# Four graph layers on one core: layer 0's table as two half precision terms, its destination one-hots in bfloat16, slots found for 64 edge tiles at once

## The chip, the cores and the metric

The kernel runs on one core of one Trainium2 chip. The time is that of one launch on the device, in microseconds (us), the median over several executions. The page of the profile is made from one execution that the hardware profiler recorded. The engines are named as the profile names them: PE does the matmuls (PEld its weight loads), DVE is the vector engine, ACT the scalar engine, POOL the general engine, and SP issues most of the transfers.

## The reference

12500 nodes with 96 features, 200000 edges sorted by destination, four layers one after the other, each followed by a residual and a layer norm. The change touches layer 0 alone:

```python
def _L0_gnn_ref(x, src, dst, W_self, W_neigh, b):
    msg = x[src]
    neigh_sum = jax.ops.segment_sum(msg, dst, num_segments=n)
    deg = jax.ops.segment_sum(jnp.ones(src.shape, x.dtype), dst, num_segments=n)
    h_neigh = neigh_sum / jnp.maximum(deg, 1.0)[:, None]
    return x @ W_self + h_neigh @ W_neigh + b
...
x = _layernorm(x + _L0_gnn_ref(x, src, dst, ...), axis=-1)
x = _layernorm(x + _L1_gnn_ref(x, ..., src, dst), axis=-1)              # two rounds of sums over edges
x = _layernorm(x + _L2_gnn_ref(x, edge_index, edge_attr_96, ...), axis=-1)  # attention over edges
x = _layernorm(x + _L3_gnn_ref(x, src, dst, ...), axis=-1)              # softmax over the edges of a node
```

## The kernel before

Nodes are cut into 98 tiles of 128 (NB) and edges, in the order of their destinations, into 1563 tiles of 128 (NT). For layer 0 the kernel multiplies first and sums later: `l0_nodes` computes x @ W_neigh for every node and keeps it on the chip as a table in bfloat16, each row as three terms (high part, rest, rest of the rest) beside one another, 288 columns (W3). The own part goes to DRAM in float32.

The sums over edges are matmuls with one-hot matrices. For the first 72 node tiles (NS) each edge is given a slot: the slots of a node tile are arranged so that 25 groups (SQ) of 128 slots hold its edges, and so that each run of 32 slots (GR) reads from one tile of the source table. `edge_steps` finds the slots of 32 edge tiles at a time: a scan over the edges (L1005), a batch of 16 small steps (L1021 to L1052), then, for 16 tiles each (CH), one-hots `A` (L1063), `oq` and products `R` (L1065 to L1075), and matmuls that put everything into its place (L1084). The result is copied from PSUM by ACT (`placed`, L1091).

`expand` adds the two halves of a node tile's slots (`lo`, L1098) and sends the row of sources to DRAM, from where it comes back spread over all partitions (`bc`). From that `one_hots` builds the source one-hot `ohT` in fp8, on DVE for even tiles (L1137) and on ACT in two passes for odd ones (L1134, L1135). `destinations` builds the destination one-hot `ohd` in fp8 on DVE (L1122). Both are also written to DRAM by SP's queue, since the later layers load them again instead of building them.

`first_sums` uses them: `gather` multiplies the table's rows by `ohT`, four matmuls of 32 columns of weights for each group of slots, cut further where a row of 288 crosses a PSUM bank (L1222), and ACT casts the result to bfloat16 messages (L1225 for two banks, L1226 for the third). `scatter`, one turn later, multiplies by `ohd` and adds up (L1234). After the last group of a node tile 25 matmuls with a column of ones count the degrees (L1240). `done` reduces the three terms (L1394), copies the degree (L1399), and for four tiles together `l0_stage` finishes the layer and makes the next layer's table.

The last 26 node tiles go by edges instead (`by_edges`): POOL fetches each edge's row by an indirect transfer (L1299), DVE builds one-hots (L1280), PE sums (L1285). They are interleaved with the 72.

The loop in `passes` sets the order in which instructions are traced: a block of slots, node batches, then as many steps of `first_sums` and `by_edges` as the slots allow. In this stage the order on each engine is then chosen when the kernel is built, by a scheduler with estimated durations; at run time every engine and every queue goes through its list in order.

Layers 1 and 3 run in `whole_pass` with the stored one-hots (L1351 gather, L1354 cast, L1360 scatter); the attention has lines of its own, among them L1546, a one-hot in fp8 on ACT, and L1576 and L1578, which take the exponential of 32 values and write 32 scaled values into every 13th place of a tile (`m[:, :n, :, HD]`).

At the end a flag is worked out from the number of edges found and from `over`; where it is set, a general version of the whole kernel runs afterwards.

Of the kernel before, what the change touches and what calls it, by code (L numbers as in the profile page):

```python
# [23 lines left out]
P = 128  # L24
# [499 lines left out]
W3 = 3 * D  # L524
# [8 lines left out]
UE = 4  # L533

# [6 lines left out]
def gnn_fast(  # L541
# [21 lines left out]
    ident_b = const.tile([P, P], BF16, name="ident_b")  # L563
    nc.vector.tensor_copy(ident_b, ident)
# [40 lines left out]
    tabs_d = [dram.tile([NB * P, 2 * D if i else W3], F16 if i else BF16, name=f"tab_d{i}") for i in range(3)]  # L605
# [22 lines left out]
    nc.vector.tensor_add(w_l0[:D, :D], w_l0[:D, :D], ident[:D, :D])  # L628
    w_kvq = weights("w_kvq", [(Wk, bk), (Wv, bv), (Wq, bq)])
# [33 lines left out]
    over = const.tile([P, NB + 4], F32, name="over")  # L663
# [62 lines left out]

    spare = {}
# [15 lines left out]

    def split(work, v, n, to, engine):

        nc.scalar.copy(to[:, :, 0, :], v)
        r = work.tile([P, GB, D], F32, name="sq")
        nc.vector.tensor_sub(r[:, :n, :], v, to[:, :, 0, :])
        engine.tensor_copy(to[:, :, 1, :], r[:, :n, :])
        engine.tensor_sub(to[:, :, 2, :], r[:, :n, :], to[:, :, 1, :])  # L750
# [38 lines left out]
    def l0_nodes(work, psum, pieces):  # L789
# [3 lines left out]
        for g, n in node_batches():  # L793
# [8 lines left out]
            to = pieces[g // CT][:, g % CT : g % CT + n].rearrange("p g (t w) -> p g t w", t=3)  # L802
            for k in range(0, n, 2):
                m = min(2, n - k)
                p = psum.tile([P, 2, 2 * D], F32, name="tp")
                for i in range(m):
                    nc.tensor.matmul(p[:, i, :], xT[:, k + i, :], w_l0, start=True, stop=True)
                nc.vector.tensor_copy(own[:, k : k + m, :], p[:, :m, :D])
                split(work, p[:, :m, D:], m, to[:, k : k + m], nc.vector)
# [177 lines left out]
    def edge_steps(c, work, psum, t0):  # L987

        n2 = min(2 * CH, TS - t0)
        c0 = t0 % BL  # L990

        pr = psum.tile([P, 3, 2 * CH], F32, name="pr")
        for i0 in range(0, n2, CH):
# [7 lines left out]
            cnt = work.tile([P, CH * P], BF16, name="cnt", bufs=1)  # L1001
# [14 lines left out]
        def small(name, dtype=F32, bufs=1):  # L1016
            return work.tile([P, 2 * CH], dtype, name=name, bufs=bufs)[:, :n]
# [6 lines left out]
        full = work.tile([P, 2 * CH + 1], F32, name="full")  # L1024
        if t0:
            nc.vector.tensor_copy(full[:, 0:1], c.full[:, 2 * CH :])
# [28 lines left out]
        for i0 in range(0, n2, CH):  # L1055
# [6 lines left out]
            A = work.tile([P, P, CH], BF16, name="A", bufs=1)  # L1062
            nc.vector.tensor_tensor(A[:, :, :n], c.iota_p[:, :, :n], pb[:, 0, None, :n].to_broadcast([P, P, n]), op=ALU.is_equal)  # L1063
            oq = work.tile([P, 2, SQ, CH], BF16, name="oq", bufs=1)
# [4 lines left out]
            R = work.tile([P, 2, 2 * SQ + 1, CH], BF16, name="R", bufs=1)  # L1069
            for k in range(2):  # L1070
                nc.vector.tensor_mul(
                    R[:, :, k * SQ : (k + 1) * SQ, :n], oq[:, :, :, :n],
# [3 lines left out]
                R[:, :, 2 * SQ, :n], oq[:, :, SQ - 1, :n], c.shi[:, None, cs].to_broadcast([P, 2, n])  # L1076
            )
            for i in range(n):
# [9 lines left out]
                if t == last:  # L1088

                    two = work.tile([P, 2, 2 * SQ + 1], F32, name="placed", bufs=4)  # L1090
# [4 lines left out]
    def expand(work, psum, placed, d):  # L1095

        lo = work.tile([P, 2 * SQ + 1], F32, name="lo", bufs=3)
        nc.vector.tensor_add(lo, placed[d][:, 1, :], placed[d + 1][:, 0, :])  # L1098
# [8 lines left out]
            s, lo[:SPARE, 2 * SQ :], float(P), lo[:SPARE, SQ - 1 : SQ], op0=ALU.mult, op1=ALU.add  # L1107
# [4 lines left out]
        return lo  # L1112
# [6 lines left out]
    def destinations(work, d, lo):  # L1119

        ohd = work.tile([P, SQ, P], FP8, name="ohd", bufs=2)
        nc.vector.tensor_tensor(  # L1122
            ohd, iota_b[:, None, :].to_broadcast([P, SQ, P]), lo[:, SQ : 2 * SQ, None].to_broadcast([P, SQ, P]),
            op=ALU.is_equal, saturate=False,
        )
        nc.sync.dma_start(ohd_d[d], ohd.rearrange("p q e -> p (q e)"))
        return ohd

    def one_hots(work, d, bc):

        o = work.tile([P, SD], FP8, name="ohT0", bufs=2)
        if d % 2:

            nc.scalar.activation(bc, bc, AF.Square, bias=less)  # L1134
            nc.scalar.activation(o, bc, AF.Relu, bias=1.0, scale=-1.0, saturate=False)  # L1135
# [37 lines left out]
    def granule(at, ohs, sp, q, j, half=0):  # L1173

        if q == SQ - 1 and j < 2:
            c = half * SPARE + j * GR
            return (ident_b if sp.dtype == BF16 else ident_h)[:, c : c + GR], sp
# [4 lines left out]
    UN = 5  # L1182
    UW = UN * W3
    BANK = UW // 3

    def pieces_of(i):

        c = i * W3
        while c < (i + 1) * W3:
            e = min((i + 1) * W3, (c // BANK + 1) * BANK)  # L1190
            yield c // BANK, c % BANK, c - i * W3, e - i * W3
            c = e

    def first_sums(work, msgp, psum, at, table, placed, done):


        ones = msgp.tile([P, 1], BF16, name="ones", bufs=1)
        nc.vector.memset(ones, 1.0)
# [13 lines left out]
        def gather(d, q0):  # L1212
            ohs, _, sp = got[d]
            m = msgp.tile([P, UW], BF16, name="msg")
            two = psum.tile([P, 2, 512], F32, name="two")
            one = psum.tile([P, 512], F32, name="one")
            banks = [two[:, 0], two[:, 1], one]
            for i in range(UN):
                for k, c, w0, w1 in pieces_of(i):
                    for j in range(NG):  # L1220
                        a, b = granule(at, ohs, sp, q0 + i, j)
                        nc.tensor.matmul(  # L1222
                            banks[k][j * GR : (j + 1) * GR, c : c + w1 - w0], a, b[:, w0:w1], start=True, stop=True
                        )
# [630 lines left out]
```

## Time and profile before

| | |
|---|---|
| median of 17 runs | 8192.24 us (8169.2 to 8227.15) |
| the profiled execution | 8200.78 us, span of its instructions 8199.0 us |
| mean granted PE clock | 0.724 |
| busy over the span | PE 5017.6 us (61%), DVE 4432.3 (54%), POOL 3786.8 (46%), ACT 2838.8 (35%) |
| layer 0's sums | from about 250 us to 2007 us, where L1351 begins |

A line of a group reads: source line, engine, operation, output <- inputs, shapes, count | busy us, mean ns of one | idle us of the engine just before them, and what ended it. Durations of neighbouring instructions on one engine overlap a little. A line of a stretch reads: its bounds, its length, then busy us (and count) of PE, PEld, DVE, ACT and POOL, the granted PE clock, the DMA share and GB/s; asked for one source line, it shows that line alone.

### The profile page before, as it was taken

To read this page: it belongs to the slowest core of one execution; us is meant where nothing else is said; L and a number is where in the kernel's file an instruction comes from. 1 tells how busy PE (TensorE), PEld (TensorE's weight loads), DVE (VectorE), ACT (ScalarE), POOL (GpSimd) and SP (SyncE) were. 2 spreads that over 40 slices of the span, in tenths; PEclk is the share of its full clock that TensorE was granted. 3 is DMA by queue.
4 is the path that set the end of the run, shared out by engine and by line. 5 is a ranking of instruction groups with operands and counts; after the bars stand their busy time and mean duration, and the time that the engine had idled before them with its cause. 6 is when DMAs were issued, how large, how long until landed. Compare 5 with 4: busy or idle time off the path is not lost.

```text
span 8199.0 us, 140834 instructions
## 1 busy us (share of the span) xinstructions
PE 5017.6 (61%) x56203; PEld 3430.8 (42%) x56203; DVE 4432.3 (54%) x9374; ACT 2838.8 (35%) x5232; POOL 3786.8 (46%) x3641
## 2 busy tenths in 40 slices
PE   4477778776466664666735555555555537666666
PEld 2345555544344442444424444444444423222323
DVE  8367777775233342444536666666666644444445
ACT  0244444444122231332323444444444423222223
POOL 0233445443444425444356666666666634443442
PEclk9677777777677776777856666666666658777778
DMA  3444444444333342344444444444444443223222
GB/s 94 123 137 147 148 148 155 149 148 127 79 95 96 96 127 75 109 112 108 118 114 127 133 133 131 131 131 131 131 130 134 133 121 85 83 83 83 83 82 62
DMA packets 697249, 949.10 MB, mean 116 GB/s; under 512 B 399450, under 2 KB 489645, under 8 KB 696581
## 3 DMA queue, kind: packets, MB, share of 16 engines
q1 hardware_dynamic: 515222, 631.37, 25.3%
q0 software_dynamic: 150624, 295.17, 14.6%
q10 hardware_dynamic: 30735, 13.47, 0.7%
q8 instruction: 443, 7.26, 0.4%
q14 instruction: 225, 1.84, 0.1%
HBM read 804.38 MB, written 135.22 MB: 115 GB/s over the span
## 4 chain that ended last, share of the span: by engine, by line
PE 20%; another core or an unknown queue 15%; DVE 13%; issue 9%; POOL 4%; ACT 1%; DMA 1%; DVEq 0%; SPq 0%; ACTq 0%; POOLq 0%
PE rows L1351 7%; PE acc L1360 5%; POOL kv L1518 4%; PE acc L1285 3%; DVE ohe L1595 2%; DVE s L1565 2%; DVE sc L1567 2%; DVE mh L1589 2%; PE acc L1611 2%; PE ep L1556 2%; DVE s L1564 1%; DVE msg L1354 1%; PE tp L1467 1%; DVE m L1579 1%
## 5 line engine op out<-in xcount | busy, mean ns | idle before, releaser
L1518 POOL DMA_INDIRECT kv<-kv_d,cols x1563 | 1570.8, 1005 | 875.4 <-issue 444.8
L1299 POOL DMA_INDIRECT rows_e<-tab_d,cols x1257 | 1390.9, 1107 | 872.3 <-PE acc L1285 514.1
L1351 PE MATMUL rows<-tab,ohT 128*32 128x192 f16 (+1 forms) x19992 | 1029.8, 303 | 1065.8 <-issue 689.8
L1354 ACT CAST msg<-rows 128x768 f16<-128x768 f32 (+1 forms) x1320 | 810.8, 639 | 2261.5 <-remote 1274.6
L1354 DVE CAST msg<-rows 128x768 f16<-128x768 f32 x660 | 630.4, 955 | 1776.3 <-remote 932.8
L1351 PEld LDWEIGHTS <-ohT 128*32 128x32 fp8e4 x19992 | 503.6, 102 | 1532.0 <-issue 1484.7
L1611 PE MATMUL acc<-mh,ohe 128*128 128x208 f16 x3115 | 518.4, 333 | 975.8 <-DVE ohe L1595 799.7
L1360 PE MATMUL acc<-msg,ohd 128*128 128x192 f16 (+1 forms) x5100 | 815.5, 301 | 123.7 <-issue 121.7
L1299 POOL DMA_INDIRECT rows_e<-ex_d,cols x611 | 590.2, 966 | 602.7 <-PE acc L1285 428.9
L1611 PEld LDWEIGHTS <-ohe 128*128 128x128 bf16 x3115 | 360.4, 134 | 1078.7 <-DVE ohe L1595 856.8
L1556 PE MATMUL ep<-w_e,attr 97*128 97x96 f32 x3126 | 625.8, 358 | 52.8 <-issue 42.0
L1360 PEld LDWEIGHTS <-ohd 128*128 128x128 fp8e4 x5100 | 446.4, 106 | 442.9 <-issue 391.0
L1556 PEld LDWEIGHTS ep<-w_e,attr 97*128 97x128 f32 x3126 | 585.3, 274 | 67.6 <-issue 61.0
L1576 ACT ACTIVATE ex<-sc 128x32 f32<-128x32 f32 x391 | 89.6, 229 | 1423.7 <-DVE sc L1568 1197.0
L1285 PE MATMUL acc<-rows_e,ones_e 128*128 128x192 f16 (+2 forms) x3660 | 513.7, 293 | 27.4 <-DVE ones_e L1280 17.8
L1225 ACT CAST msg<-two 128x960 bf16<-128x960 f32 x360 | 344.9, 958 | 460.2 <-PE two L1222 255.1
L1564 DVE TENSOR_TENSOR s<-ep,kv 128x384 f32<-128x384 f32 x391 | 215.7, 552 | 527.1 <-remote 366.4
L1158 POOL DMA_INDIRECT spare<-tab_d,spare_i x72 | 124.4, 1728 | 718.7 <-DMA rowd<-lorow 248.7
L1285 PEld LDWEIGHTS <-ones_e 128*128 128x128 bf16 x3660 | 371.8, 116 | 133.0 <-DVE ones_e L1280 24.7
L1565 DVE TENSOR_TENSOR s<-s,qp 128x384 f32<-128x384 f32 x391 | 216.5, 554 | 385.0 <-remote 287.0
L1560 PE MATMUL qp<-qs,ohq 128*128 128x96 f16 x3126 | 312.2, 244 | 182.4 <-issue 181.3
L1167 POOL DMA_INDIRECT spare<-tab_d,spare x72 | 69.3, 962 | 757.2 <-PE rows L1351 610.6
(922 smaller groups left out, 8651.4 us busy)
## 6 DMA issues: line engine op xcount, KB each, us to landing
ohT<-ohT_d SPq DMA_DIRECT2D x204, 400.0 KB
ohd<-ohd_d SPq DMA_DIRECT2D x204, 400.0 KB
attr<-cols_edge_attr_dram SPq DMA_DIRECT2D x390, 192.0 KB
bc<-rowd SPq DMA_DIRECT2D x72, 800.0 KB
qb<-qrow SPq DMA_DIRECT2D x97, 512.0 KB
sb<-srow SPq DMA_DIRECT2D x72, 512.0 KB
cb<-crow SPq DMA_DIRECT2D x72, 512.0 KB
ohd_d<-ohd SPq DMA_DIRECT2D x72, 400.0 KB
```

The source lines that it names most:

```text
L1225: nc.scalar.copy(m[:, : 2 * BANK].rearrange("p (b w) -> p b w", b=2), two[:, :, :BANK])
L1285: nc.tensor.matmul(acc[:, : W + count], ones[:, :, i], rows_of[u][:, i, : W + count], start=(t + i == first), stop=(t + i == last),)
L1299: nc.gpsimd.indirect_dma_start(out=m[:, i, :W], out_offset=None, in_=table, in_offset=bass.IndirectOffsetOnAxis(ap=rest_src[:, t : t + 1], ...
L1351: nc.tensor.matmul(ps[j * GR : (j + 1) * GR, i // R, i % R * W : (i % R + 1) * W], a, b, start=True, stop=True)
L1354: (nc.scalar.copy if engine else nc.vector.tensor_copy)(m, ps[:, :, : R * W])
L1360: nc.tensor.matmul(acc[d][:, :W], got[d][1][:, q, :], m, start=(q == 0), stop=(q == SQ - 1))
L1518: nc.gpsimd.indirect_dma_start(out=kv[:, i, :], out_offset=None, in_=kv_d, in_offset=bass.IndirectOffsetOnAxis(ap=cols[:, t0 + i : t0 + i ...
L1556: nc.tensor.matmul(ep[:, i, :], a[:, i * P : (i + 1) * P], w_e, start=True, stop=True)
L1560: nc.tensor.matmul(qp[:, i, :], ohq[:, i * P : (i + 1) * P], qs[:, t * D : (t + 1) * D], start=(t == 0), stop=(t == 1))
L1564: nc.vector.tensor_mul(s[:, :n, :], ep[:, :n, :], kv[:, :n, :D])
L1565: nc.vector.tensor_mul(s[:, :n, :], s[:, :n, :], qp[:, :n, :])
L1611: nc.tensor.matmul(acc[d].rearrange("p t w -> p (t w)"), ohe[:, k * P : (k + 1) * P, i], m[:, i].rearrange("p t w -> p (t w)"), start=(t = ...
```

## The change

The table of layer 0 becomes two terms in half precision (192 columns, `halves_of`), after W_neigh is multiplied by 64 (L0); the degree's reciprocal takes the factor out. `split` goes. ACT sums the squares of each row into `l0_ss`, and at the end the flag is also set where such a sum lies below 1 and is not 0, or is 2^30 or more.

`gather` takes four groups of slots at a time, then two, in turn, into PSUM tiles of two banks and of one, with one ACT cast each into message tiles that have a column of ones behind each row; `scatter` then counts the degrees in the same matmul (193 columns). The degree is copied by ACT.

`destinations` compares in bfloat16, five groups of slots (QG) at a time, the group innermost, and the scatter reads its weights from there at steps of five elements. Five ACT copies per tile turn these into fp8 in the old order, for DRAM. The two ACT passes of the odd source one-hots are cut into five pieces each.

`edge_steps` takes 64 edge tiles (GE); `cnt`, `A`, `oq` and `R` get two buffers, `placed` nine for four, and R's columns change places so that the two halves of `lo` are added by two instructions (`lo` in float32, `lod` in bfloat16). The loop in `passes` runs 26 node batches and four steps of `first_sums` a turn. The ring of `by_edges` in this stage has 9 buffers for 10.

```diff
@@ -531,6 +530,9 @@
+QG = 5
+L0 = 2.0**6
+GE = 4 * CH
@@ -602,7 +602,7 @@
-    tabs_d = [dram.tile([NB * P, 2 * D if i else W3], F16 if i else BF16, name=f"tab_d{i}") for i in range(3)]
+    tabs_d = [dram.tile([NB * P, 2 * D], F16, name=f"tab_d{i}") for i in range(3)]
@@ -626,6 +626,7 @@
+    nc.vector.tensor_scalar(w_l0[:, D:], w_l0[:, D:], L0, None, op0=ALU.mult)
@@ -799,14 +797,18 @@
             own = work.tile([P, GB, D], F32, name="own")
-            to = pieces[g // CT][:, g % CT : g % CT + n].rearrange("p g (t w) -> p g t w", t=3)
+            to = pieces[g // CT][:, g % CT : g % CT + n].rearrange("p g (t w) -> p g t w", t=2)
             for k in range(0, n, 2):
...
                 nc.vector.tensor_copy(own[:, k : k + m, :], p[:, :m, :D])
-                split(work, p[:, :m, D:], m, to[:, k : k + m], nc.vector)
+                halves_of(p[:, :m, D:], to[:, k : k + m])
+                for i in range(m):
+                    junk = work.tile([P, D], BF16, name="junk")
+                    at = g + k + i
+                    nc.scalar.activation(junk, p[:, i, D:], AF.Square, accum_out=l0_ss[:, at : at + 1])
             nc.sync.dma_start(rows(own_d[0], g, n), own[:, :n, :])
@@ -986,10 +988,10 @@
-        n2 = min(2 * CH, TS - t0)
+        n2 = min(GE, TS - t0)
...
-        pr = psum.tile([P, 3, 2 * CH], F32, name="pr")
+        pr = psum.tile([P, 3, GE], F32, name="pr")
@@ -1014,16 +1016,16 @@
-            return work.tile([P, 2 * CH], dtype, name=name, bufs=bufs)[:, :n]
+            return work.tile([P, GE], dtype, name=name, bufs=bufs)[:, :n]
...
-        full = work.tile([P, 2 * CH + 1], F32, name="full")
+        full = work.tile([P, GE + 1], F32, name="full")
...
-            nc.vector.tensor_copy(full[:, 0:1], c.full[:, 2 * CH :])
+            nc.vector.tensor_copy(full[:, 0:1], c.full[:, GE:])
@@ -1059,21 +1061,21 @@
-            A = work.tile([P, P, CH], BF16, name="A", bufs=1)
+            A = work.tile([P, P, CH], BF16, name="A", bufs=2)
...
-            oq = work.tile([P, 2, SQ, CH], BF16, name="oq", bufs=1)
+            oq = work.tile([P, 2, SQ, CH], BF16, name="oq", bufs=2)
...
-            R = work.tile([P, 2, 2 * SQ + 1, CH], BF16, name="R", bufs=1)
-            for k in range(2):
+            R = work.tile([P, 2, 2 * SQ + 1, CH], BF16, name="R", bufs=2)
+            for k, at in enumerate((0, SQ + 1)):
...
-                    R[:, :, k * SQ : (k + 1) * SQ, :n], oq[:, :, :, :n],
+                    R[:, :, at : at + SQ, :n], oq[:, :, :, :n],
...
-                R[:, :, 2 * SQ, :n], oq[:, :, SQ - 1, :n], c.shi[:, None, cs].to_broadcast([P, 2, n])
+                R[:, :, SQ, :n], oq[:, :, SQ - 1, :n], c.shi[:, None, cs].to_broadcast([P, 2, n])
@@ -1087,15 +1089,17 @@
-                    two = work.tile([P, 2, 2 * SQ + 1], F32, name="placed", bufs=4)
+                    two = work.tile([P, 2, 2 * SQ + 1], F32, name="placed", bufs=9)
...
-        lo = work.tile([P, 2 * SQ + 1], F32, name="lo", bufs=3)
-        nc.vector.tensor_add(lo, placed[d][:, 1, :], placed[d + 1][:, 0, :])
+        lo = work.tile([P, SQ + 1], F32, name="lo", bufs=2)
+        nc.vector.tensor_add(lo, placed[d][:, 1, : SQ + 1], placed[d + 1][:, 0, : SQ + 1])
+        lod = work.tile([P, SQ], BF16, name="lod", bufs=4)
+        nc.vector.tensor_add(lod, placed[d][:, 1, SQ + 1 :], placed[d + 1][:, 0, SQ + 1 :])
@@ -1118,21 +1122,25 @@
-        ohd = work.tile([P, SQ, P], FP8, name="ohd", bufs=2)
-        nc.vector.tensor_tensor(
-            ohd, iota_b[:, None, :].to_broadcast([P, SQ, P]), lo[:, SQ : 2 * SQ, None].to_broadcast([P, SQ, P]),
-            op=ALU.is_equal, saturate=False,
-        )
-        nc.sync.dma_start(ohd_d[d], ohd.rearrange("p q e -> p (q e)"))
-        return ohd
+        o = work.tile([P, SQ // QG, P, QG], BF16, name="ohd", bufs=2)
+        ohd = work.tile([P, SQ // QG, QG, P], FP8, name="ohd_8", bufs=2)
+        for g in range(SQ // QG):
+            nc.vector.tensor_tensor(
+                o[:, g], c5, lo[:, None, g * QG : (g + 1) * QG].to_broadcast([P, P, QG]), op=ALU.is_equal
+            )
+            nc.scalar.activation(ohd[:, g].rearrange("p q e -> p e q"), o[:, g], AF.Copy, saturate=False)
+        nc.sync.dma_start(ohd_d[d], ohd.rearrange("p g q e -> p (g q e)"))
+        return o
...
-            nc.scalar.activation(bc, bc, AF.Square, bias=less)
-            nc.scalar.activation(o, bc, AF.Relu, bias=1.0, scale=-1.0, saturate=False)
+            for c in range(0, SD, SD // 5):
+                b = bc[:, c : c + SD // 5]
+                nc.scalar.activation(b, b, AF.Square, bias=less)
+                nc.scalar.activation(o[:, c : c + SD // 5], b, AF.Relu, bias=1.0, scale=-1.0, saturate=False)
         else:
@@ -1209,51 +1211,53 @@
-        def gather(d, q0):
...
-        def scatter(d, q0, m):
...
+        def gather(now, banks):
+            ps = psum.tile([P, banks, 512], F32, name=f"rows{banks}")
+            m = msgs[banks].pop(0)
+            msgs[banks].append(m)
+            for i, (d, q) in enumerate(now):
+                ohs, _, sp = got[d]
+                for j in range(NG):
+                    a, b = granule(at, ohs, sp, q, j)
+                    nc.tensor.matmul(
+                        ps[j * GR : (j + 1) * GR, i // R, i % R * W : (i % R + 1) * W], a, b, start=True, stop=True
+                    )
+            n = -(-len(now) // R)
+            nc.scalar.copy(
+                m[:, : n * R, :W].rearrange("p (b r) w -> p b r w", r=R),
+                ps[:, :n, : R * W].rearrange("p b (r w) -> p b r w", r=R),
+            )
+            return [(d, q, m[:, i, : W + 1]) for i, (d, q) in enumerate(now)]
+        def scatter(d, q, m):
+            if q == 0:
...
+            g, i = divmod(q, QG)
+            nc.tensor.matmul(acc[d][:, : W + 1], got[d][1][:, g, :, i], m, start=(q == 0), stop=(q == SQ - 1))
+            if q == SQ - 1:
...
+        items = [(d, q) for d in range(NS) for q in range(SQ)]
+        waiting, u, banks = [], 0, 2
+        while u < len(items):
+            now = items[u : u + R * banks]
+            for d, q in now:
+                if q == 0:
+                    yield
+                    fetch(d + 1)
+            waiting.append(gather(now, banks))
+            u += R * banks
+            banks = 3 - banks
+            if len(waiting) > 1:
+                for w in waiting.pop(0):
+                    scatter(*w)
+        for ws in waiting:
+            for w in ws:
+                scatter(*w)
@@ -1396,7 +1400,7 @@
-                nc.vector.tensor_copy(deg[:, d : d + 1], acc[:, at : at + 1])
+                nc.scalar.copy(deg[:, d : d + 1], acc[:, at : at + 1])
@@ -1750,32 +1754,32 @@
                 tabp = c2.enter_context(tc.tile_pool(name="f_tab", bufs=1))
-                spare["ring"] = spares(tabp, W3, BF16, "spare")
+                spare["ring"] = spares(tabp, 2 * D, F16, "spare")
                 blk = c2.enter_context(tc.tile_pool(name="s_blk", bufs=2))
...
                 psum = c2.enter_context(tc.tile_pool(name="f_psum", bufs=1, space=PSUM))
-                pieces, at = new_table(tabp, W3, BF16)
+                pieces, at = new_table(tabp, 2 * D, F16)
                 nodes = l0_nodes(work, psum, pieces)
-                sums = first_sums(work, msgp, psum, at, tabs_d[0], c.placed, in_batches(l0_stage, terms=(3,), count=True))
+                sums = first_sums(work, msgp, psum, at, tabs_d[0], c.placed, in_batches(l0_stage, count=True))
                 next(sums)
                 others = by_edges(
-                    rest, msgp, psum, work, tabs_d[0], in_batches(l0_stage, terms=(3,), count=True, name="sums_e"), 10, count=True
+                    rest, msgp, psum, work, tabs_d[0], in_batches(l0_stage, count=True, name="sums_e"), 9, count=True
                 )
...
                 turn = 1 - AHEAD
-                for k, t0 in enumerate(range(0, TS, 2 * CH)):
+                for k, t0 in enumerate(range(0, TS, GE)):
                     if t0 % BL == 0:
...
                     edge_steps(c, step, psum, t0)
-                    for _ in range(13):
+                    for _ in range(26):
                         next(nodes, None)
...
-                    while turn + 2 <= 2 * k:
+                    while turn <= min(4 * k, NS - 2):
                         next(sums)
                         turn += 1
-                        while k and made * NS <= turn * 4 * (NB - NS):
+                        while made * NS <= turn * 4 * (NB - NS):
                             next(others)
@@ -1802,6 +1806,13 @@
+        low = work.tile([P, 2, NB], F32, name="low")
+        nc.vector.tensor_scalar(low[:, 0], l0_ss, 1.0, None, op0=ALU.is_lt)
+        nc.vector.scalar_tensor_tensor(low[:, 1], l0_ss, 0.0, low[:, 0], op0=ALU.is_gt, op1=ALU.mult)
+        nc.vector.tensor_reduce(over[:, NB + 1 : NB + 2], low[:, 1], AX.X, ALU.max)
+        nc.vector.tensor_scalar(low[:, 0], l0_ss, 2.0**30, None, op0=ALU.is_lt)
+        nc.vector.tensor_reduce(low[:, 1, 0:1], low[:, 0], AX.X, ALU.min)
+        nc.vector.tensor_scalar(over[:, NB + 2 : NB + 3], low[:, 1, 0:1], -1.0, 1.0, op0=ALU.mult, op1=ALU.add)
```

## The prediction

> **What bounds the kernel now.** I read the page first: the span is 8199.0 us, and no engine is busy throughout. The sums of layer 0 run while the slots are still being found, from the first gathers at about 250 us to 2007 us, where the next layer's matmuls begin. All of the change lies there. The stretches of that stage come next:
>
> ```profile
> 410.00:1850.00 1440.00, 1115.10 (x14883) 728.24 (x14880) 1096.77 (x2184) 693.75 (x950) 625.63 (x421) 0.77 0.47 147
> 600.00:1850.00 1250.00, 970.56 (x12871) 631.69 (x12870) 965.73 (x1912) 599.48 (x823) 563.89 (x370) 0.76 0.48 149
> ```
>
> Columns after the length: PE, weight loads, DVE, ACT, POOL, then granted clock, DMA share, GB/s. From 600 to 1850 us the line that builds the destination one-hots runs 54 times, once for a node tile, so a tile takes 1250 / 54 = 23.15 us. In it PE is busy 17.97 us, DVE 17.88, ACT 11.10. Two engines share the load and each idles 5.2 us per tile for the other. The groups of lines of that stretch:
>
> ```profile
> L1225 ACT CAST msg<-two 128x960 bf16<-128x960 f32 x269 | 257.7, 958 | 339.8 <-PE two L1222 205.2 <-remote 55.5 <-PE one L1222 36.6
> L1122 DVE TENSOR_TENSOR ohd<-iota_b,lo 128x3200 fp8e4<-128x3200 bf16 x54 | 187.9, 3479 | 19.6 <-PE acc L1240 17.4 <-PE one L1222 1.8 <-PE two L1222 0.2
> L1226 ACT CAST msg<-one 128x480 bf16<-128x480 f32 x269 | 151.5, 563 | 40.8 <-remote 16.3 <-PE one L1222 15.4 <-PE pr L1023 3.8
> L1063 DVE TENSOR_TENSOR A<-iota_p,pb 128x2048 bf16<-128x2048 bf16 x52 | 63.4, 1219 | 41.6 <-PE place L1084 29.5 <-PE acc L1285 8.1 <-issue 2.5
> L1098 DVE TENSOR_TENSOR lo<-placed 128x51 f32<-128x51 f32 x52 | 10.7, 207 | 97.3 <-ACT placed L1091 84.3 <-issue 13.0
> ```
>
> Of DVE's 284 us idle, 97.3 stand before L1098 and 41.6 before L1063: DVE waits for PE's placing matmuls, which queue behind gathers. PE's weight on this stage comes from the three-term table; the later layers do the same work with two terms. Matmul lines alone, in the order L1222, L1234, L1285 (this stage), then L1351, L1360, L1285 (a layer with 192 columns):
>
> ```profile
> 600.00:1850.00 1250.00, 328.79 (x7536) 186.45 (x7535) 0.76 0.48 149
> 600.00:1850.00 1250.00, 277.29 (x1345) 127.07 (x1345) 0.76 0.48 149
> 600.00:1850.00 1250.00, 116.71 (x608) 74.57 (x608) 0.76 0.48 149
> 2300.00:3690.00 1390.00, 417.88 (x9619) 243.84 (x9618) 0.75 0.38 102
> 2300.00:3690.00 1390.00, 307.33 (x2410) 215.56 (x2410) 0.75 0.38 102
> 2300.00:3690.00 1390.00, 103.56 (x1077) 91.30 (x1078) 0.75 0.38 102
> ```
>
> **PE, per tile.** Gather: 140 matmuls at 43.6 ns become 100 at 43.4: -1.8 us. Scatter: 25 at 206 ns become 25 at 127.5: -2.0. The 25 one-column degree matmuls (49.8 us for 1350, 37 ns each) go: -0.9. Edge sums: 11.3 matmuls fall from 192 to 96 ns: -1.1. The stationary one-hots are now read at steps of 5 elements; L1285 already reads at steps of 4 and shows no loss. PE goes to 12.2 us.
>
> **DVE, per tile.** The one-hot of 3479 ns becomes five of 640 bf16 elements. The same operation on 512 elements (L1280) takes 414 ns and on 2048 (L1063) 1219, so 0.52 ns an element and 483 ns for 640: 2.4 us, -1.1. Those rows have runs of 4 and 16, none has 5. The other bound is the float tensor operation, 352 ns for 192 columns and 552 for 384, so 819 ns for 640: 4.1 us, +0.6. I take the former, as L1280 is the nearest row.
>
> The Trainium skill speaks against it: VectorE: DVE Perf Modes, section "Mode 2×_1P", wants pairs that start at a multiple of 4 bytes, and every second group of five starts 2 bytes past one; by it the five would cost as the float rows do. Its page Vector Engine (DVE) Microarchitecture Reference, section 5.1, finds that alignment makes no difference; no row here shows such a start.
>
> The 16 small steps of a slot batch (138 to 275 ns each) run once for 64 edge tiles instead of 32; they start some 0.10 us apart, so half of them, less the added width, is -0.45. The degree copy leaves for ACT (-0.2), the reduction shrinks from 442 to 351 ns (-0.1), one more 51-column addition of 0.2. DVE: 16.2 us (17.9 by the other bound).
>
> **ACT, per tile.** Its rows elsewhere in the trace:
>
> ```profile
> L1354 ACT CAST msg<-rows 128x768 f16<-128x768 f32 x660 | 527.8, 800 | 613.1 <-remote 431.0 <-PE rows L1351 136.8 <-issue 25.7
> L1354 ACT CAST msg<-rows 128x384 f16<-128x384 f32 x660 | 316.0, 479 | 1648.4 <-remote 843.6 <-PE rows L1351 673.8 <-issue 100.0
> L1546 ACT ACTIVATE ohq<-qb 128x512 fp8e4<-128x512 bf16 x390 | 246.0, 631 | 14.7 <-DMA q_d<-q 2.4
> L1576 ACT ACTIVATE ex<-sc 128x32 f32<-128x32 f32 x390 | 89.4, 229 | 1422.6 <-DVE sc L1568 1195.9 <-issue 138.3 <-DVE sc L1567 51.7
> L1578 ACT ACTIVATE m<-ex 128x32 f32<-128x32 f32 x390 | 100.7, 258 | 12.4
> L1578 ACT ACTIVATE m<-ex 128x24 f32<-128x24 f32 x1 | 0.2, 243 | 0.0
> ```
>
> Message casts: 7.6 us now; 25 rows in turns of four and two make 4.17 pairs of 800 + 479 ns, 5.3 us: -2.25. New are five casts of the one-hots to fp8 for the later layers. They read 640 bf16 elements in order and write each 128 bytes from the last. Written in order, L1546 (523 ns at 384 elements, 0.84 ns each) gives 738 ns. But L1578 writes one element in 13 and goes from 243 to 258 ns over 8 elements, 1.88 ns each, where L1576, in order, shows 0.75. So 640 x 1.88 + 198 = 1.40 us. I take 1.40, as its step is the nearer case: 7.0 us a tile (3.7 by the other). Single bytes might cost more; that end is a rival.
>
> The Trainium skill's ScalarE: Activation LUTs, section "What ACT_TABLE_LOAD costs", gives 0.833 ns an element for every function; by it a cast would be about 0.72 us, an estimate that puts ACT back by 3.4 us a tile. Its SBUF — State Buffer, under "Door 1: The DMA port swizzle", holds that each access to a new 16-byte line pays a penalty, which agrees with L1578.
>
> Cutting the odd tiles' two passes into five pieces each adds eight fixed costs, 0.8 us a tile; degree copies 0.3. ACT: 11.1 - 2.25 + 7.0 + 0.8 + 0.3 = 16.95 us. It becomes the longest.
>
> **New waits.** An fp8 cast waits for its DVE piece, a degree copy for PE's last scatter. Behind both in ACT's queue stand message casts, for which PE's next gather waits, and the copies of the placed slots, for which DVE waits. The bf16 one-hot buffer now comes free only after cast and scatter. On SP's queue the write of the fp8 one-hots waits for ACT instead of DVE, and the loads of sb, cb and bc stand behind it. I leave all this inside the idle term below; a stall of 1 us a tile would cost 62 us.
>
> **Sum.** Idle per tile was 5.26 us of DVE. A second buffer for A and its kin takes the 0.77 before L1063. The wait before L1098 comes once a batch, half as often: -0.9. The remaining 2.7 I shrink by a quarter, as PE's work falls by a third. That leaves 2.9. Pace: 16.95 + 2.9 = 19.85 us, 3.3 less than 23.15. The even stretch of 1440 us holds 62.2 tiles: -205 us. Start: the 25 node batches run as a chain over one PSUM buffer, free when its last reader ends. The two squares per half batch stand where a subtraction stood: the 246 ns of a 96-column read each, or twice that with an accumulator read, against 351: +7 to +32 us over 49 halves, taken as +15. The two DVE operations that go were off that chain. The 32 edge tiles more ahead of the first gather are 25 us of DVE, counted at nothing since DVE sits idle 70 us between 332 and 408 us; uncovered, they cost 25. Ring depth 9 for 10: nothing, POOL waits 260 us for PE there anyway. Constants, ones and the guards at the end: +1. Together -189 against the profiled execution's 8200.78 us (span 8199.0): 8012. The median of the 17 runs is 8.5 lower, so 8003.
>
> **Rivals.**
> 1. *ACT casts cheap, DVE the bound.* At 3.7 us for the casts ACT has 13.65, DVE 16.2; with 2.9 idle 19.1 us, -252 us, 7940. With still better overlap, 7850. For it: the casts can run whenever ACT is free. Against: L1578.
> 2. *Little overlap.* The idle stays at 5.2 us: 22.15 us a tile, -46 us, 8150. For it: two engines again carry nearly equal loads, as now, and the order within each queue is fixed beforehand by estimates. Against: PE's slack of a third.
> 3. *Slower: ACT becomes a wall.* Byte-wise strided writes cost more than 4-byte ones. With 2.9 idle the pace passes 23.15 when ACT reaches 20.25, that is when a cast takes 2.06 us, 2.9 ns an element. At 2.3 us the tile takes 24.35: +75 us and the start's +16, 8283. PE then waits for casts in ACT's queue. Against: 1.5 times the one strided row.
> 4. *No such path.* If the new range guard fired, the general path would run as a whole and the time would multiply. Row sums of squares lie near 96 x 64² for these inputs, far from 1 and from 2^30; no chance is given.
>
> **Numbers.** Forecast 0.48, rival 1 0.24, rival 2 0.11, no change 0.04, rival 3 0.13. About 0.2% (16 us) is what can be told from no change. Faster 0.83, same 0.04, slower 0.13. Range 7850 to 8190: it takes in rivals 1 and 2 and leaves out most of rival 3.
>
> **What would show it.** Right: PE's busy share of the stage near 60%, the new casts at 1.2 to 1.6 us, one-hot pieces near 0.48 us, the next layer beginning near 1820 us, later stages unchanged. Wrong: casts near 0.75 us (then DVE bounds it, rival 1); casts over 2 us, or PE waiting mostly for ACT (rival 3); one-hot pieces near 0.82 us; a first gather later by more than 40 us.

## The result: slower by 9.4%, and the profile after

The changed kernel takes 8964.25 us (8953.21 to 8981.06) against 8192.24 before (47 runs by now, the same median): a ratio of 1.0941, with the 95% interval in brackets here and below [1.0926, 1.0956]. The forecast was 8003 us; the range of 7850 to 8190 does not hold the result. The profiled execution takes 8954.09 us (span 8952.3). The stage is where the time went: the first gather starts at 391.9 us instead of 253.5, and the next layer's matmuls at 2766.9 instead of 2007.0, 760 us later; the stages behind it are as long as they were.

The kernel before itself took 6054 to 6066 us in three of the five sets of runs told of below and 8191 to 8294 us in the other two, as in the first result, so every ratio is to the runs of before of its own set, and the set's level (the median of before) is given with it; what makes the two levels no run here shows.

The stretch of 1800 us in which the destination one-hots of 54 node tiles are built, first all instructions and then the matmul lines L1222 (gather), L1236 (scatter) and L1289 (sums by edges); columns as before:

```profile
600.00:2400.00 1800.00, 871.88 (x9418) 538.33 (x9411) 866.99 (x1878) 1295.55 (x1307) 477.78 (x381) 0.59 0.32 99
600.00:2400.00 1800.00, 294.55 (x5472) 126.90 (x5464) 0.59 0.32 99
600.00:2400.00 1800.00, 279.77 (x1368) 153.35 (x1368) 0.59 0.32 99
600.00:2400.00 1800.00, 105.19 (x640) 72.57 (x640) 0.59 0.32 99
```

A tile takes 1800 / 54 = 33.3 us instead of 23.15. ACT is busy 24.0 us of it, DVE 16.06, PE 16.1. The granted clock is 0.59; it was 0.76. The groups of that stretch:

```profile
L1131 ACT ACTIVATE ohd<-ohd 128x640 fp8e4<-128x640 bf16 x270 | 787.1, 3266 | 31.1 <-DVE ohd L1128 28.2 <-DVE full L1032 1.5 <-issue 0.9
L1226 ACT CAST msg<-rows 128x768 f16<-128x768 f32 x229 | 193.6, 846 | 210.3 <-PE rows L1222 104.0 <-remote 47.1 <-PE acc L1289 42.0
L1226 ACT CAST msg<-rows 128x384 f16<-128x384 f32 x228 | 118.3, 519 | 62.1 <-remote 32.2 <-PE rows L1222 13.6 <-PE acc L1289 8.3
...
L1128 DVE TENSOR_TENSOR ohd<-c,lod 128x640 bf16<-128x640 bf16 x270 | 134.1, 549 | 56.4 <-PE acc L1236 30.2 <-PE rows L1222 15.5 <-remote 6.5
```

The new copy, L1131, lasts 3.27 us where 1.40 was forecast. Neighbours overlap a little, so the five hold ACT for 787.1 / 54 = 14.6 us a tile. What PE waited for in the stretch (us, times, longest):

```profile
PE acc L1236 <- ACT msg L1226: 374.6, 75, 16.3
PE acc L1236 <- ACT deg L1403: 164.0, 13, 16.8
PE acc L1289 <- ACT deg L1403: 144.5, 12, 16.6
```

Together 683 us, 12.6 us a tile. In the kernel before, PE's waits for message casts came to 65 us in the 1250 us of its stretch, 1.2 us a tile; the two longest lines:

```profile
PE two L1222 <- ACT msg L1225: 50.1, 60, 3.7
PE one L1222 <- ACT msg L1226: 12.0, 6, 4.9
```

In the changed kernel neither cast nor degree copy takes long; they stand behind the five copies, as the order in time shows (ACT's rows first, then PE's):

```profile
1542.07 14.46 ACT L1131 ACTIVATE ohd<-ohd 128x640 fp8e4<-128x640 bf16 x5 [0.16 <-DVE ohd L1128]
1556.04 0.81 ACT L1226 CAST msg<-rows 128x384 f16<-128x384 f32 x1
1556.76 0.15 ACT L1403 COPY deg<-acc 128x1 f32<-128x1 f32 x1
...
1544.45 0.23 PE L1025 MATMUL pr<-ovf,ones_b 128*128 128x64 bf16 x1
1556.90 0.48 PE L1236 MATMUL acc<-msg,ohd 128*128 128x193 f16 x2 [12.21 <-ACT deg L1403]
```

PE stands still for 12.21 us until ACT is through. An ACT that is busy for only 72% of the stretch is therefore the wall here: for more than half of its idle time (277 of some 500 us) it waits for PE, which it has kept waiting. That shorter copies take the loss away, the experiments have to show.

### The profile page after: what moved, and what is told of

It reads as the page before. It is cut to its first block, busy times and chain, and to the rows that moved or that the text cites. A ratio compares the mean times of both kernels' runs of the same rounds, so it can differ in the third digit from the quotient of the medians.

```text
span 8952.3 us, 132169 instructions
## 1 busy us (share of the span) xinstructions
PE 4895.6 (55%) x51487; PEld 3314.8 (37%) x51487; DVE 4315.6 (48%) x9256; ACT 3792.0 (42%) x6054; POOL 3685.1 (41%) x3644
## 4 chain that ended last, share of the span: by engine, by line
PE 17%; another core or an unknown queue 11%; issue 11%; POOL 9%; DVE 9%; ACT 1%; DMA 1%; DVEq 0%; SPq 0%; POOLq 0%; ACTq 0%
POOL kv L1522 9%; PE rows L1355 6%; PE acc L1364 5%; PE acc L1289 3%; DVE msg L1358 1%; DVE s L1569 1%; DVE ohe L1599 1%; DVE sc L1571 1%; DVE mh L1593 1%; PE tp L1471 1%; PE ep L1560 1%; DVE s L1568 1%; PE acc L1615 1%; ACT msg L1358 1%
## 5 line engine op out<-in xcount | busy, mean ns | idle before, releaser
L1303 POOL DMA_INDIRECT rows_e<-tab_d,cols x1257 | 1269.5, 1010 | 1041.5 <-PE acc L1289 674.7
L1131 ACT ACTIVATE ohd<-ohd 128x640 fp8e4<-128x640 bf16 x360 | 1050.5, 3261 | 40.6 <-DVE ohd L1128 36.1
L1236 PE MATMUL acc<-msg,ohd 128*128 128x193 f16 x1800 | 367.1, 330 | 756.8 <-ACT msg L1226 491.6
L1166 POOL DMA_INDIRECT spare<-tab_d,spare_i x72 | 143.3, 1990 | 1359.8 <-PE rows L1222 960.8
L1289 PE MATMUL acc<-rows_e,ones_e 128*128 128x192 f16 (+2 forms) x3660 | 496.4, 287 | 218.4 <-ACT deg L1403 163.4
L1226 ACT CAST msg<-rows 128x768 f16<-128x768 f32 x600 | 398.1, 682 | 393.8 <-PE rows L1222 189.7
L1236 PEld LDWEIGHTS <-ohd 128*128 128x128 bf16 x1800 | 201.2, 131 | 871.3 <-issue 858.4
L1289 PEld LDWEIGHTS <-ones_e 128*128 128x128 bf16 x3660 | 363.4, 117 | 329.6 <-issue 243.4
```

Source lines behind the costliest of these rows:

```text
L1131: nc.scalar.activation(ohd[:, g].rearrange("p q e -> p e q"), o[:, g], AF.Copy, saturate=False)
L1226: nc.scalar.copy(m[:, : n * R, :W].rearrange("p (b r) w -> p b r w", r=R), ps[:, :n, : R * W].rearrange("p b (r w) -> p b r w", r=R),)
L1236: nc.tensor.matmul(acc[d][:, : W + 1], got[d][1][:, g, :, i], m, start=(q == 0), stop=(q == SQ - 1))
L1289: nc.tensor.matmul(acc[:, : W + count], ones[:, :, i], rows_of[u][:, i, : W + count], start=(t + i == first), stop=(t + i == last),)
L1303: nc.gpsimd.indirect_dma_start(out=m[:, i, :W], out_offset=None, in_=table, in_offset=bass.IndirectOffsetOnAxis(ap=rest_src[:, t : t + 1], ...
```

## The experiments

**The copy by itself** (level 6064). The kernel before, with a prologue that makes copies of 640 elements in eight forms on ACT and three on DVE, six times each.

> The kernel before with eleven forms of a 640-element copy from bf16 put ahead of it, six times each; only their durations are of interest. ACT: fp8 in order; fp8 written at 128 bytes (the change's form); fp8 written at 5 bytes; fp8 in order read at 10 bytes; fp8 written at 4 bytes; bf16 at 128 bytes; bf16 at 4 bytes; float at 128 bytes. DVE: fp8 at 128 bytes; fp8 in order; fp8 in order read at 10 bytes. Theory 'distance': what counts is that each write goes to another place, so fp8, bf16 and float at 128 bytes cost alike (3.0 to 3.4 us) and fp8 at 4 or 5 bytes is near 0.74. Theory 'single bytes': fp8 costs 3 us at every step over one, and bf16 and float at 128 bytes cost 1.2 to 1.5 us, as the 4-byte row with a step of 52 bytes did (1.88 ns an element).

Groups of the prologue, by form:

```profile
L610 ACT ACTIVATE m_8b<-m_in 128x640 fp8e4<-128x640 bf16 x6 | 18.2, 3031 | 0.0
L614 ACT ACTIVATE m_2a<-m_in 128x640 bf16<-128x640 bf16 x6 | 18.1, 3024 | 0.0
L611 ACT ACTIVATE m_8c<-m_in 128x640 fp8e4<-128x640 bf16 x6 | 8.3, 1380 | 0.0
L616 ACT ACTIVATE m_4a<-m_in 128x640 f32<-128x640 bf16 x6 | 7.5, 1254 | 0.0
L615 ACT ACTIVATE m_2b<-m_in 128x640 bf16<-128x640 bf16 x6 | 7.2, 1202 | 0.0
L613 ACT ACTIVATE m_8e<-m_in 128x640 fp8e4<-128x640 bf16 x6 | 5.4, 903 | 0.0
L612 ACT ACTIVATE m_8d<-m_in 128x640 fp8e4<-128x640 bf16 x6 | 5.2, 873 | 0.0
L609 ACT ACTIVATE m_8a<-m_in 128x640 fp8e4<-128x640 bf16 x6 | 4.3, 722 | 0.0
```

In order (L609) a copy takes 0.72 us. Written 128 bytes apart, fp8 (L610) and bf16 (L614) take 3.03 us, float32 (L616) 1.25. At 4 or 5 bytes (L613, L615, L611) it is 0.90 to 1.38; read at steps of 10 bytes and written in order (L612), 0.87. So neither theory holds as stated: it is not the distance alone, since float32 is cheap at it, and not single bytes, since bf16 costs the same as fp8. What was dear in these forms is an element of one or two bytes written 128 bytes from the last one. The three forms at 128 bytes also differ in how many elements are written before the pattern comes back beside the first (5 in fp8, 10 in bf16, 20 in float32); 5 and 10 cost the same, but no form tries one width with another count, so why float32 is spared stays open. On DVE the same fp8 copies take 1.80 us at 128 bytes (L618) and 0.68 in order (L619).

**The copies in order, and none** (level 6064). Three ways to take the strided write away:

```diff
 e1_read_step: order kept, the copy reads at a step
-            nc.scalar.activation(ohd[:, g].rearrange("p q e -> p e q"), o[:, g], AF.Copy, saturate=False)
+            nc.scalar.activation(ohd[:, g], o[:, g].rearrange("p e q -> p q e"), AF.Copy, saturate=False)
 e2_in_order: fp8 kept with the group innermost; the later layers read their weights at steps of 5 bytes
-        ohd = work.tile([P, SQ // QG, QG, P], FP8, name="ohd_8", bufs=2)
+        ohd = work.tile([P, SQ // QG, P, QG], FP8, name="ohd_8", bufs=2)
...
+            nc.scalar.activation(ohd[:, g], o[:, g], AF.Copy, saturate=False)
...
 e3_dve_fp8: destinations as in the kernel before, one DVE instruction, no copy on ACT
```

> The changed kernel, but each fp8 copy of a destination one-hot walks its output in order (group, then node) and reads its bf16 input at steps of five elements; every value and every other instruction is the same. Theory 'step write': the 3.27 us of a copy come from writing 128 bytes away at each element; the copy falls to 0.7 to 0.9 us, ACT's load to about 12.5 us a node tile, the pace to 19 or 20 us, the time to 7930 to 8020 us. Rival 'transposed access': going against the layout costs the same on the read side; the copy stays above 2 us and the time above 8500. Rival 'the rest': the copies are not what holds the stage (degree copies on ACT, the 64-tile batches, the new order); the copy gets short but the time stays above 8250.

> The changed kernel, but the fp8 one-hots are stored with the group innermost, as the bf16 ones are, so the copies read and write in order; the later layers read their weights out of them at steps of five bytes. 'Step write': a copy takes about 0.74 us (the 0.84 ns an element of the in-order fp8 row), the stage as in the run that reads at steps, 7930 to 8020 us if the later layers do not mind. If weight loads at a step of five bytes cost PE anything, the scatter of layers 1 and 3 (5100 matmuls) shows it: 10 ns each would be 50 us. 'The rest': above 8250 whatever the copies cost.

> The changed kernel with one part undone: the destination one-hot is built in fp8 by one DVE instruction as before (3.48 us), no bf16 copy, no ACT copy; the scatter reads fp8 weights in order. 'Step write': DVE goes from 16.1 to about 17 us a tile, ACT falls to about 9, the pace is 20 to 21 us, the time 8000 to 8090 us. 'The rest': above 8250.

Measured: 1.0012 [1.0002, 1.0021], 0.995 [0.9934, 0.9967] and 0.9941 [0.9924, 0.9957]. The copies take 0.92 us (e1) and 0.73 us (e2) in the stage. All three are rid of the loss; none brings the 1 to 3% that the theory still expected. The change itself was not in this set; in later sets it lies 0.093 above e2 (level 8294) and at 1.115 (level 6054). So the strided write is the loss, and a second step of the prediction is wrong besides: what ought to be gained once it is cheap.

**The change beside parts of it** (level 8191).

```diff
 a_change: the changed kernel
 e4_in_order_32: as e2_in_order, with GE = 2 * CH and the loop in passes of the kernel before
 e6_before_64: the kernel before with n2 = min(GE, TS - t0), GE = 4 * CH and the changed loop; ring 9,
               nine buffers of `placed`
 e7_terms_only: as e3_dve_fp8, with GE = 2 * CH and the loop of before, the degree copied by DVE,
                and the two ACT passes of the odd source one-hots uncut; turns of four and two,
                degrees counted in the scatter and all buffers as in the change
```

> The changed kernel itself, beside the kernel before on the chip that takes 6064 us for the latter. Theory (the strided fp8 copies make ACT a wall): five copies of 3.27 us instead of 0.73 add 12.7 us of ACT to a node tile, whose ACT work was 13 us with copies in order (696 us for 54 tiles), so 26 us a tile against the pace of 19.3 with copies in order; over some 70 tiles +450 to +650 us: 6480 to 6680 us, ratio 1.07 to 1.10. Rival (the other chip's long gaps between PE's instructions did it, the copies run beside other work): 6070 to 6200, ratio 1.00 to 1.02.

> Copies in order, as before in the run of that name, but slots found for 32 edge tiles at a time and the loop of the kernel before. Theory (the batch of 64 starts the sums late: first gather at 377 us against 253, with DVE busy 34 to 48% from 200 to 400 us): the first gather returns to 250 to 270 us and 60 to 124 us of the stage come back, less some 10 to 30 us of small DVE steps: 5930 to 5990 us, ratio 0.978 to 0.988. Rival (what is waited for at the start is worked off later anyway): 6010 to 6060, ratio 0.991 to 1.0.

> The kernel before with only the slots found for 64 edge tiles at once (loop and copies of the placed slots as in the change; the ring of the sums by edges 9 for 10). Theory (late start): first gather near 377 us for 253, +50 to +110 us: 6110 to 6175 us, ratio 1.008 to 1.018. Rival (the halved number of small steps pays it back): 6030 to 6075, ratio 0.994 to 1.002.

> The two half precision terms alone: destinations in fp8 by DVE, degree copy on DVE, odd source one-hots in two uncut passes, 32 edge tiles at a time. Theory (DVE, 18.1 of 21.0 us a tile in the kernel before on this chip, stays the bound): the pace goes to some 20 us, 40 to 80 us less: 5980 to 6025 us, ratio 0.987 to 0.994. Rival (PE was the bound there): PE falls by 3 to 5 us a tile and the pace follows it, 120 us or more: below 5940, ratio below 0.98.

The change again: 1.0954 [1.0924, 1.0983]; its theory and rival were meant for the other level, where it is 1.115 (below), more than either. Slots for 64 edge tiles alone: 1.0088 [1.006, 1.0116], as the theory had it, with the first gather at 354.4 us for 253.5 and the stage's end at 2061 for 2007. So the start is late by the larger batch with its loop, and over half of that is never made up. Back at 32 tiles with copies in order, the first gather is at 268.8 us, but the ratio is 0.9944 [0.9925, 0.9963]: the rival's range. A tile takes 22.1 us (52 in 1150 us) with ACT at only 12.8. The two terms with little else: 0.9858 [0.9826, 0.989], 8067.41 us for 8190.86: between the theory's 0.987 and the rival's 0.98, and at this level the 123 us saved are as many as the rival asked for. This version beats both kernels. A tile (53 in 1150 us) takes 21.7 us with DVE at 17.8, so DVE idles 3.9 us for the 5.3 of before; in e4 it idles 22.1 - 16.4 = 5.7. The stretches of e4 and e7:

```profile
600.00:1750.00 1150.00, 815.23 (x9025) 509.40 (x9017) 854.85 (x2044) 665.04 (x1246) 496.64 (x362) 0.64 0.47 147
600.00:1750.00 1150.00, 817.08 (x9254) 538.28 (x9254) 941.13 (x1926) 484.53 (x726) 607.96 (x357) 0.65 0.48 152
```

**Is 7 us of copies cheap enough?** (level 8294). The change and e2, e3 again in one set, and e2 with each copy made twice, so that the five pairs take 7.3 us of ACT, near the 7.0 that the prediction gave the copies.

```diff
+            for _ in range(2):
+                nc.scalar.activation(ohd[:, g], o[:, g], AF.Copy, saturate=False)
```

> The changed kernel again, to stand beside copies in order in one set of runs. Theory (strided copies): ratio to before 1.09 to 1.10 where before takes some 8190 us, with ACT's copies at 3.2 to 3.3 us and 24 us of ACT to a node tile; where before takes some 6064 us, 1.07 to 1.11. Rival (copies hurt only where PE's instructions come slowly): 1.00 to 1.03 where before takes 6064 us.

> Copies in order with 64 edge tiles, a second time, for the comparison with the same kernel at 32 edge tiles (0.9944 in the set before) and with the strided copies. Theory (the late start costs some 54 us net, as the slots alone did, and the strided write costs the rest): ratio 0.998 to 1.006, so 0.09 or more below the changed kernel. Rival (the larger batch pays for its start): 0.990 to 0.996.

> Copies in order, but each of the five made twice, so that ACT's copies take some 7.3 us of a node tile, what the prediction gave them (7.0). Theory (ACT has room for that, only the 16 us were too many): 0 to 0.013 above the ratio of the run with copies made once. Rival (any further 3.6 us in ACT's queue delays the message casts for which PE waits): 0.017 to 0.03 above it.

> Destinations in fp8 by DVE in one instruction, no copies on ACT, the rest as changed, a second time. Theory (with copies in order either engine may do this work): within 0.005 of the ratio of the run with copies in order. Rival (ACT's copies delay messages even in order): lower than it by over 0.006.

Measured: 1.0911 [1.0881, 1.0941], 0.9982 [0.9969, 0.9996], 1.0207 [1.0178, 1.0236] and 0.9925 [0.9899, 0.9951]. The strided write is worth 0.093 of before. The second copies, 3.65 us of ACT a tile by their durations (ACT is busy 3.0 us longer, as neighbours overlap), cost 0.0225, the rival's value. e3 lies 0.0057 below e2, between theory and rival. The stretches from 600 to 1750 us, copies once and twice (255 and 235 one-hot pieces, so 51 and 47 tiles):

```profile
600.00:1750.00 1150.00, 807.31 (x8770) 501.33 (x8763) 820.95 (x1778) 645.23 (x1214) 481.68 (x348) 0.63 0.46 144
600.00:1750.00 1150.00, 730.29 (x7997) 454.21 (x7997) 768.11 (x1661) 737.01 (x1349) 423.85 (x312) 0.61 0.42 132
```

With ACT at 737.01 / 47 = 15.7 us, DVE at 16.3 and PE at 15.5, a tile takes 24.5 us. At this level the kernel is slower than before even at about the price that I gave the copies. Beside e3, which leaves ACT free of them, building the destinations in bf16 and copying gains nothing: e2 is 0.0057 slower here and the same within the noise at 6064.

**Where the idle time comes from** (level 6066; the last two in a set at 6054).

```diff
 e9_no_copies: as e2_in_order, without the copies; zeros are stored for the later layers
 e10_spread: the changed kernel, its five strided copies traced one after each gather
+        late.extend((copy, g) for g in range(SQ // QG))
...
             waiting.append(gather(now, banks))
+            if late:
+                f, g = late.pop(0)
+                f(g)
...
 e11_spread_in_order_32: the same in e4_in_order_32
 e12_gather_twice: as e2_in_order, every matmul of the gather made twice
```

> The kernel with copies in order (64 edge tiles), without the copies: a tile of zeros goes to DRAM in place of the fp8 destinations, so the later layers add up with zeros; their instructions are the same. Theory (time in ACT's queue passes to the pace even below ACT's limit; the second set of copies cost 0.0225): ratio 0.973 to 0.988, 0.010 to 0.025 below copies in order (0.9982). Rival (as long as ACT has room its copies are free): 0.994 to 1.0.

> The changed kernel with its strided copies unchanged in price, but traced one after each gather instead of five in a row. Theory (PE waits for message casts behind blocks of 16 us): ACT's 24 us a tile stay, its idle 9 us shrink to 2 to 4: 5 to 7 us a tile less, ratio 1.03 to 1.06. Rival (the sum of ACT's time and the same idle set the pace wherever the copies stand): 1.08 to 1.10.

> Copies in order, 32 edge tiles at a time, the copies one after each gather. Theory (blocks delay the casts): 0.005 to 0.015 below the 0.9944 of the same kernel with five in a row: 0.979 to 0.989. Rival (3.6 us in a row are short enough for the two message buffers ahead): 0.992 to 0.997.

> Copies in order (64 edge tiles), each gather's matmuls made twice into the same place: 100 more per node tile, 4.3 to 5.4 us of PE. Theory (PE is slow because it idles: the granted clock rises with its load and pays part of it, and PE is not the wall): granted clock of the stage above 0.68 against 0.63, ratio 0 to 0.012 above copies in order (0.9982). Rival (PE's time is on the path): 0.02 to 0.045 above it.

> The changed kernel, beside the same with its copies spread. Theory (the sum of ACT's time sets the pace): within 0.010 of the spread kernel's ratio in this set; where before takes some 6066 us, 1.095 to 1.112. Rival (blocks of five): 0.015 to 0.05 above the spread kernel's ratio, so 1.117 to 1.15 where before takes 6066 us.

> Strided copies one after each gather, beside the changed kernel. Theory (sum of ACT's time): within 0.010 of the changed kernel's ratio in this set. Rival (blocks of five): 0.015 to 0.05 below it; where before takes 8190 us or more, 1.04 to 1.08.

Without copies: 0.989 [0.9874, 0.9907], 0.006 below e2 at this level (another set), between the two expectations. Spread: 1.1023 [1.1004, 1.1041], just above the rival's range, and beside the change itself 1.1036 [1.1018, 1.1055] against 1.115 [1.1132, 1.1169]. Standing in a row thus costs 0.0114, 67 us, again between theory and rival; the other nine tenths of the loss (the change is 0.120 above e2 at this level) stay when the copies are spread. There ACT is busy 23.5 of 27.6 us a tile (38 in 1050 us of the first spread run), which fits the theory that the sum of ACT's time sets the pace; no other place for the copies was tried. Its stretch:

```profile
600.00:1650.00 1050.00, 621.99 (x6416) 383.98 (x6415) 582.89 (x1298) 891.20 (x896) 355.55 (x257) 0.57 0.36 112
```

Spread and in order at 32 tiles: 0.9901 [0.9885, 0.9918], between its expectations; e4 was not run at this level.

The doubled gather: 1.0095 [1.0079, 1.0112], 0.0145 above e2 at this level. Its gather line from 600 to 1650 us, then that of e2:

```profile
600.00:1650.00 1050.00, 377.90 (x10052) 239.28 (x10048) 0.78 0.51 160
600.00:1650.00 1050.00, 277.69 (x5448) 120.62 (x5448) 0.66 0.53 167
```

A matmul takes 37.6 ns in the one and 51.0 in the other: with more to do PE was granted a clock of 0.78 for 0.66, and 100 more matmuls a tile lengthened the tile by about 1.5 us (20.8 for 19.3). PE's busy time is no fixed price. The cost lies a little above the theory's 0.012 and below the rival's 0.02; the clock is what the theory said.

## Why the prediction was wrong, step by step

- **The price of a copy (failed).** "I take 1.40, as its step is the nearer case": measured 3.27 us. L1578's row is float32; at 128 bytes float32 does take 1.25 us, but fp8 3.03. I carried the step over and not the width, and put "byte-wise strided writes" with the rivals. The five hold ACT 14.6 us instead of 7.0: +7.6 us a tile. The Trainium skill's ScalarE: Activation LUTs, section "What ACT_TABLE_LOAD costs", with 0.833 ns an element for every function, fits the copies in order (0.72 us measured; the estimate was about 0.72) and is too low by a factor of four for the strided ones, where the measurement decides. The 16-byte line of its SBUF — State Buffer, "Door 1: The DMA port swizzle", would charge float32 and bf16 at 128 bytes alike; measured are 1.25 and 3.02.
- **The idle term (failed).** "Idle 2.9", shrunk because PE's work falls by a third. ACT idles 33.3 - 24.0 = 9.3 us: +6.4 us a tile. This term fails without the strided write too. Beside DVE, the longest engine there, 24.5 - 16.3 = 8.1 us of idle time are left with copies at about the predicted price (e8), and 22.5 - 16.1 = 6.4 with copies in order (e2 in the same set). In e7, where PE is relieved and ACT gets no copies, it is 3.9, a quarter below before. So the relief of PE may well shrink the wait, as the forecast had it; what the forecast left out is that work added to ACT lengthens it (6.4 to 8.1 from e2 to e8), since PE, ACT and DVE wait for one another in turn. At the level of 6064 the wait is about 3 us in either kernel (before with the prologue 21.0 - 18.1, e2 19.3 - 16.0). "A stall of 1 us a tile would cost 62 us" was the right price; the stall was taken too small.
- **The other ACT work (right).** 24.0 - 14.6 = 9.4 us against 9.95.
- These three give the pace: 19.85 + 7.6 + 6.4 - 0.55 = 33.3 us; the idle term is what the others leave of it, so the sum fits by its making. Over 62.2 tiles the error of 13.5 us is 840 of the 942 us by which the profiled execution missed.
- **The start (failed).** +15 forecast; the first gather came 138 us later, past the mark of 40 that the text set. The 32 more edge tiles were "counted at nothing". e6 shows 101 us of delay by the batch with its loop, 54 of which are left at the stage's end. The +15 itself, for the squares, was about right: e7, which has them and 32 edge tiles, starts 9 us after before (262.9).
- **PE (failed).** 12.2 us forecast, 16.1 measured. Counts fell as told, but a gather matmul takes 53.8 ns for 43.4, a scatter 204.5 for 127.5, an edge sum 164 for 96. The forecast priced them from stages at a granted clock of 0.75; here it is 0.59, a factor of 1.27. That covers the gather (1.24), but not the scatter (1.60) and the edge sum (1.71). A scatter takes 176 ns in e12 too, at 0.78, and 174 in e3, with fp8 weights in order at 0.70; so the later layers' 127.5 ns did not carry over to this stage at any clock seen, and why stays open. e12 shows the clock rising when PE gets more to do, and that PE is not the bound: 100 more matmuls cost about 1.5 us a tile.
- **DVE (right).** 16.06 against 16.2; the comparisons of five groups run at 549 ns each (520 to 590), near the 483 taken and not the 819 of the other bound. The Trainium skill's VectorE: DVE Perf Modes, section "Mode 2×_1P", with its starts at multiples of 4 bytes, is not borne out here.
- **Rival 3 was the mechanism**, though not for single bytes alone (bf16 costs the same), and its point of decision, 2.06 us a copy, was passed. Its price of 8283 us at 2.3 us a copy was too low by the idle term: by the same rule 3.27 us would have given some 8580.

Two slips in the sums bear on nothing: rival 1's 7940 leaves out the start's 16 us that rivals 2 and 3 have, and -0.45 for the small steps is more than half of 16 steps at 0.10 us over two tiles (0.40).

Open: why 3.65 us of ACT cost 0.0225 at the level of 8294 and the same amount only 0.006 at 6064 to 6066; the doubled copies ran at the one level and the omitted ones at the other.

## What to carry to other kernels

A price from a strided row holds for its element width as well as its step: copy the very form into a prologue before a loop is built on it, or write in order and let the reader take the step. Where engines wait for each other in turn, added work on one of them is not free because it is below the pace: take the wait per turn as it is in the profile, and ask what stands behind the new instructions in their queue. A matmul's duration is read together with the granted clock of its stretch, and the clock can move with the change: 0.76 to 0.59 here, where PE came to wait for ACT. What sets it these runs do not show: with the copies spread PE was busy for more of its time than in the change (59% for 50%, in one set), and was granted 0.57 for 0.62.

## What the runs showed of the hardware

Not expected was the jump between widths at one distance: 640 elements written 128 bytes apart cost ACT 1.25 us in float32 and 3.02 to 3.03 in bf16 and fp8. Nor that reading at a step costs so little (0.87 us against 0.72), nor that stationary weights read at steps of five bytes cost the later layers nothing (from the next layer's first gather to the last: 4245 us in e2 and in the kernel before with the prologue). A scatter's weights in bf16 at steps of ten bytes loaded in 131 ns, fp8 in order in 111 (e2 and e3, at granted clocks of 0.66 and 0.70; width and step are not told apart). The prediction read "no loss" off L1285, but its bf16 loads at steps of four elements took 125 ns where the scatter's fp8 took 110 (before, 600 to 1850 us).
